# Issuing three kinds of transfers from GpSimd's queue instead of SyncE's

## The chip, the cores and the metric

The kernel runs on one core of a Trainium2 chip. The metric is the device time of one execution in microseconds (us), as the median of several runs. The engines are named as in the profile: PE is TensorE (matrix multiply), PEld its weight load, DVE is VectorE, ACT is ScalarE, POOL is GpSimd and SP is SyncE. SP does no arithmetic here; it only issues transfers. ACT and POOL can issue transfers too, each on a queue of its own. SBUF is the core's on-chip memory, PSUM the small memory that PE writes to, and "DRAM" means the chip's large memory.

## The reference

The input x is 4 images of 512 channels, each 64 by 64 (f32). Two layers follow each other.

```python
# layer 0: linear attention with 64 heads of 8, with and without a convolution of q, k, v
qkv = concat(h @ wq.T, h @ wk.T, h @ wv.T)               # 1x1 projections, per pixel
pw  = grouped_1x1(depthwise_5x5(qkv))                    # a second set of q, k, v
f   = concat(qkv, pw).reshape(B, -1, 24, N)              # 128 heads, N = 4096 pixels
query, key_, value = relu(f[:, :, :8]), relu(f[:, :, 8:16]), f[:, :, 16:]
scores = einsum('bhdn,bhen->bhde', value_with_a_row_of_ones, key_)
out = einsum('bhde,bhen->bhdn', scores, query)
out = out[:, :, :-1] / (out[:, :, -1:] + EPS)            # divided by the row of ones
y = conv1x1(out, proj_kernel) * inv + shift + x

# layer 1: edge filters on y, four branches, attention over channels, fuse, norm, gelu
E = stack(sobel(y), laplace(y), diagonals(y), gradient(y))
feat = gelu(bn(einsum('kbchw,koc->bkohw', E, w_branch)))          # 4 x 128 channels
att = sigmoid(gelu(mean_hw(feat) @ w_att1.T + b_att1) @ w_att2.T + b_att2)
z = conv1x1(feat * att, w_fuse) + b_fuse
z = (z - mean_c(z)) / sqrt(var_c(z) + eps)
result = gelu(z * ln_gamma + ln_beta) + y
```

## The kernel before, in words

**The front.** For each of the 4 images there are 4 groups of 128 channels (class `Group`, 16 groups). A group makes keys, values and queries of 8 strips of 512 pixels each (`project`, L256, and `values`, L279), their attention scores, the 5 by 5 convolutions of keys and queries (`convolve`, L388, 160 small matmuls per half), and a correlation that replaces the convolution of values (`correlate`, L441). The queries are not multiplied with the scores here. They are divided by their denominators on DVE (`divide`, L378, tile `q`; `conv_divide`, L548, tile `cq`) and stored in the DRAM tensors `heads` and `cheads`, 256 KB at a time. The matrices of a convolution are built on POOL (`load_mat`, L236, tile `mat`, two buffers).

**The three stages behind.** When all four groups of an image are done, three generators work it off. `project_out` (L612, called Y below) loads the divided queries again (tile `hd`), multiplies them with the folded projection, adds x, and writes y to DRAM. `edge_branches` (L667, called E) loads windows of y (tile `win`), forms the edge maps on DVE and ACT, multiplies them with the branch weights and stores the result as `ef`. `fuse_out` (L759, called F) loads `ef` in 8 strips, four tiles of 128 channels to a strip. For each channel tile `c` its helper `fuse` (L805) does four matmuls (L808), a square on ACT (L810), the tile `z` on DVE (L812, six buffers) and, for three of four, a running sum on POOL (`total`, L815). Its helper `norm` (L817) sums the squares over channels on PE (L819), takes root and reciprocal (L821, L822), and then for each of the four tiles: loads the rows of y that are added to the result (tile `yr`, two buffers), multiplies (L829, DVE), applies gelu (L830, ACT), adds `yr` (L833, POOL), and stores the result in `out` (L834).

**What sets the order.** PE's instructions run in the order in which the program issues them (`manual_schedule`, L101). Into that order the stages behind are mixed by hand: `advance` (L881) is called after each step of the front with that step's share of time, and pulls steps of Y, E and F of the image before. So F of images 0, 1 and 2 has the front, or E of the last image, beside it, and F of image 3 stands alone at the end. In `norm`'s place in the strip loop,

```python
fuse(0, ef, zs, total)
fuse(1, ef, zs, total)
norm(j - 1, *held)
fuse(2, ef, zs, total)
fuse(3, ef, zs, total)
```

two `z` tiles of the new strip exist before the four of the old one are stored, which fills the six buffers. The third and fourth `z` of a strip can be written only when the first two stores of the strip before have landed. The other engines and queues get their order at build time, by dependences and program order. A queue works its list from the front: a transfer that waits for its data holds back all that stand behind it. Transfers wait, too, for the landing of earlier and unrelated ones on the same queue, as the waits of SP show.

Of the kernel before, what the change touches and what calls it, by code (L numbers as in the profile page):

```python
# [83 lines left out]
def conv_seq_kernel(  # L84
    ctx: ExitStack, tc, x, wqkv, dpk, wtab, proj, projc, pwk, bn0, consts, vec, watt1, batt1, watt2, wbr, wfuse, out
):
    nc = tc.nc
# [15 lines left out]
    def work_tile(name, n=512):  # L103
        return work.tile([P, 512], F32, tag="w", name=name)[:, :n]

    def ps_tile(name):
        return psum.tile([P, 512], F32, tag="ps", name=name)
# [8 lines left out]
    def rows(ap, width=W):  # L116
        return ap.rearrange("p (r c) -> p r c", c=width)
# [79 lines left out]
    def center_bias():  # L197

        fb_ps = ps_tile("fb_ps")
        nc.tensor.matmul(fb_ps[:, 0:4], lhsT=ones, rhs=vec_sb[:, V_FB, :], start=True, stop=True)  # L200
        fb_mean = const.tile([P, 1], F32, name="fb_mean")
        nc.vector.tensor_reduce(fb_mean, fb_ps[:, 0:4], AX.X, ALU.add)
        nc.vector.tensor_scalar(fb_mean, fb_mean, 1.0 / C, None, ALU.mult)
        nc.vector.tensor_scalar(fbias, vec_sb[:, V_FB, :], fb_mean, None, ALU.subtract)
# [15 lines left out]
    class Group:  # L220
# [157 lines left out]
        def divide(self, half):  # L378
            banks = self.spread_out(self.rec)
            for k in range(4):  # L380
                j = 4 * half + k
                q = work_tile("q")
                nc.vector.tensor_mul(q, self.rq.pop(j), banks[k])
                nc.sync.dma_start(out=self.heads[j, :, self.g, :], in_=q)

# [160 lines left out]
        def conv_divide(self, half):  # L548
            banks = self.spread_out(self.crec)
            for i in range(4):  # L550
                q = work_tile("cq")
                nc.vector.tensor_mul(q, self.conv[QUERY][i], banks[i])
                nc.sync.dma_start(out=self.cheads[half, self.g, i], in_=q)

# [202 lines left out]
    def fuse_out(b, efs, pool_sb, side):  # L759

        y = ys[b % 2]
        with ExitStack() as stack:
            pool = stack.enter_context(tc.tile_pool(name=f"F{b}", bufs=2, side=side, reuse_waits="tile"))
            wf_sb = pool.tile([P, NCH, C], F32, name="wf_sb", bufs=1)
            nc.sync.dma_start(out=wf_sb, in_=wfuse)
            watt1_sb = pool.tile([P, NCH, 64], F32, name="watt1_sb", tag="sq", bufs=3)
            nc.sync.dma_start(out=watt1_sb, in_=watt1)
            watt2_sb = pool.tile([64, C], F32, name="watt2_sb", tag="sq", bufs=3)
            nc.sync.dma_start(out=watt2_sb, in_=watt2)
            wf_mean = small.tile([P, NCH], F32, name="wf_mean")  # L770
            nc.vector.tensor_reduce(wf_mean, wf_sb, AX.X, ALU.add)
            nc.vector.tensor_scalar(wf_mean, wf_mean, 1.0 / C, None, ALU.mult)
            yield 0.0


            pooled = small.tile([P, 4], F32, name="pooled")
            nc.vector.tensor_reduce(pooled, pool_sb, AX.X, ALU.add)
            yield 14.0
            if b == 0:
                center_bias()  # L780
            hid_ps = ps_tile("hid_ps")
            for k in range(4):
                nc.tensor.matmul(
                    hid_ps[0:64, 0:1], lhsT=watt1_sb[:, k, :], rhs=pooled[:, k : k + 1], start=(k == 0), stop=(k == 3)
                )
            hid = small.tile([64, 1], F32, name="hid")
            nc.scalar.activation(hid, hid_ps[0:64, 0:1], AF.Gelu, bias=batt1_sb, scale=1.0 / N)
            yield 4.0
            att_ps = ps_tile("att_ps")
            for k in range(4):  # L790
                nc.tensor.matmul(att_ps[:, k : k + 1], lhsT=watt2_sb[:, ts(k, P)], rhs=hid, start=True, stop=True)
            att = small.tile([P, 4], F32, name="att")
            nc.vector.tensor_add(att, att_ps[:, 0:4], vec_sb[:, V_ATT2, :])
            nc.scalar.activation(att, att, AF.Sigmoid)

            for k in range(4):
                nc.vector.tensor_scalar(
                    wf_sb[:, k, :], wf_sb[:, k, :], wf_mean[:, k : k + 1], att[:, k : k + 1], ALU.subtract, ALU.mult
                )
            yield 8.0  # L800


            share = SHARE_F / (NJ * 5)

            def fuse(c, ef, zs, total):  # L805
                ps = ps_tile("zps")
                for k in range(4):
                    nc.tensor.matmul(ps, lhsT=wf_sb[:, k, ts(c, P)], rhs=ef[k], start=(k == 0), stop=(k == 3))  # L808
                sq = total if c == 0 else pool.tile([P, 512], F32, name="sq", tag="sq", bufs=3)
                nc.scalar.activation(sq, ps, AF.Square, bias=fbias[:, c : c + 1])  # L810
                z = pool.tile([P, 512], F32, name="z", tag="z", bufs=6)
                nc.vector.tensor_scalar(z, ps, fbias[:, c : c + 1], None, ALU.add)  # L812
                zs.append(z)
                if c:
                    nc.gpsimd.tensor_add(total, total, sq)  # L815

            def norm(j, zs, total):  # L817
                ps = ps_tile("var")
                nc.tensor.matmul(ps, lhsT=ones, rhs=total, start=True, stop=True)  # L819
                rstd = pool.tile([P, 512], F32, name="rstd", tag="rstd", bufs=1)  # L820
                nc.scalar.activation(rstd, ps, AF.Sqrt, bias=ln_eps, scale=1.0 / C)  # L821
                nc.vector.reciprocal(rstd, rstd)  # L822
                for c in range(NCH):
                    z = zs[c]
                    yr = pool.tile([P, 8 * WB], F32, name="yr", tag="yr")
                    nc.sync.dma_start(
                        out=yr, in_=y[c].rearrange("p r w -> p (r w)")[:, (8 * j + 1) * WB : (8 * j + 9) * WB]
                    )
                    nc.vector.tensor_mul(z, z, rstd)  # L829
                    nc.scalar.activation(  # L830
                        z, z, AF.Gelu, bias=vec_sb[:, V_LNB, c : c + 1], scale=vec_sb[:, V_LNG, c : c + 1]
                    )
                    nc.gpsimd.tensor_add(rows(z), rows(z), rows(yr, WB)[:, :, 1 : W + 1])  # L833
                    nc.sync.dma_start(out=out[b, c, :, ts(j, 512)], in_=z)  # L834

            held = None
            for j in range(NJ + 1):
                if j < NJ:
                    ef = []
                    for k in range(4):  # L840
                        t = pool.tile([P, 512], F32, name="ef", tag="ef", bufs=8)
                        nc.sync.dma_start(out=t, in_=efs[j][:, k, :])
                        ef.append(t)
                    zs = []
                    total = pool.tile([P, 512], F32, name="total", tag="total")
                    fuse(0, ef, zs, total)
                    yield share
                    fuse(1, ef, zs, total)
                    yield share
                else:  # L850
                    yield 6.0
                if held:
                    norm(j - 1, *held)
                    yield share
                if j < NJ:
                    fuse(2, ef, zs, total)
                    yield share
                    fuse(3, ef, zs, total)
                    yield share
                    held = zs, total  # L860
# [191 lines left out]
```

## Time and profile before

| | before |
|---|---|
| median of 3 runs | 5078.56 us (5077.92 to 5086.61) |
| the profiled execution: its own time | 5063.71 us |
| its span, first to last instruction | 5061.9 us |
| granted clock of TensorE, mean | 0.967 |
| PE busy | 4702.0 us (93%) |
| DVE busy | 2124.7 us (42%) |
| ACT busy | 1626.5 us (32%) |
| POOL busy | 392.7 us (8%), 291 instructions |
| transfers issued by SP, by ACT | q1: 758.68 MB, q10: 100.74 MB |
| F of image 0, 1, 2, 3, about | 1816 to 2070, 3140 to 3390, 4600 to 4870, 4910 to 5062 us |

The busy time of an engine is the time in which it ran instructions. A row of waits says which instruction waited, for whom, how long in total, how many times, and the longest wait. The timeline gives instructions in order of time, with the idle time before them in square brackets. Issuing a transfer is not counted as busy time; the queue SPq has rows of its own.

### The profile page before, as it was taken

The page shows a single profiled execution, that of the slowest core. Times are in us where ns is not written, and L with a number is a line of the kernel's source. Part 1 is how long each engine was busy: PE and PEld are TensorE (multiplying, and loading weights), DVE is VectorE, ACT ScalarE, POOL GpSimd, SP SyncE. Part 2 cuts the span into 40 slices and gives each one's busy share as a digit, 9 for nine tenths or more (in the row PEclk, how much of TensorE's full clock was granted, in tenths as well). Part 3 has the DMA queues.
Part 4 walks back from the last instruction along what each step waited for, and adds up shares of the span by engine and source line. Part 5 has one row for each costly group of instructions (what it writes and reads, how often), then busy time and mean ns, then how long its engine had stood idle before and what let it go on. Part 6 is the DMA issues. An engine that isn't in the chain of part 4 may idle for free. (4 is left out here: it accounts for less than half of the span.)

```text
span 5061.9 us, 107134 instructions
## 1 busy us (share of the span) xinstructions
PE 4702.0 (93%) x46362; PEld 2739.7 (54%) x46362; DVE 2124.7 (42%) x2960; ACT 1626.5 (32%) x2833; POOL 392.7 (8%) x291
## 2 busy tenths in 40 slices
PE   9999999999999999799899999899989898898777
PEld 5665654455666554454465655454456665445443
DVE  1222221116556433211455653431146557157965
ACT  2112111004444423200345442320024445035765
POOL 0000000000000013100000000310000000001335
PEclk9999999999999999899999999999999999999889
DMA  6444466666656565676555665657655553774425
GB/s 196 138 123 130 132 206 190 158 165 181 192 189 183 179 205 170 197 178 156 176 176 181 193 202 176 213 188 167 163 173 175 184 169 129 200 184 118 151 88 172
DMA packets 635945, 866.26 MB, mean 171 GB/s; under 512 B 324393, under 2 KB 395081, under 8 KB 617041
## 3 DMA queue, kind: packets, MB, share of 16 engines
q1 hardware_dynamic: 551504, 758.68, 51.8%
q10 hardware_dynamic: 83968, 100.74, 6.4%
q8 instruction: 364, 5.96, 0.5%
q14 instruction: 109, 0.88, 0.1%
HBM read 578.09 MB, written 213.98 MB: 156 GB/s over the span
## 5 line engine op out<-in xcount | busy, mean ns | idle before, releaser
L262 PE MATMUL proj<-xt,w_sb 128*128 128x512 f32 x2048 | 955.8, 610 | 52.9 <-DMA xt<-in_x 31.8
L655 PE MATMUL yps<-hd,fold_sb 128*128 128x512 f32 x2048 | 899.6, 596 | 9.7 <-DMA hd<-heads 8.7
L396 PE MATMUL cv<-inp,mat 32*32 32x512 f32 x20480 | 730.2, 597 | 35.4 <-issue 27.3
L262 PEld LDWEIGHTS proj<-xt,w_sb 128*128 128x128 f32 x2048 | 382.7, 194 | 523.3 <-issue 450.7
L655 PEld LDWEIGHTS yps<-hd,fold_sb 128*128 128x128 f32 x2048 | 384.9, 190 | 493.5 <-issue 445.3
L396 PEld LDWEIGHTS cv<-inp,mat 32*32 32x32 f32 x20480 | 420.3, 103 | 314.6 <-issue 154.2
L730 PE MATMUL br<-maps,wbr_sb 128*128 128x256 f32 x2048 | 495.0, 396 | 51.8 <-ACT maps L713 42.2
L808 PE MATMUL zps<-ef,wf_sb 128*128 128x512 f32 x1024 | 469.9, 610 | 53.5 <-DMA ef<-ef 19.0
L730 PEld LDWEIGHTS br<-maps,wbr_sb 128*128 128x128 f32 x2048 | 399.7, 198 | 165.9 <-issue 51.3
L284 PEld LDWEIGHTS val<-w_sb,xt 128*128 128x128 f32 x4096 | 470.2, 192 | 33.9 <-issue 26.1
L284 PE MATMUL val<-w_sb,xt 128*128 128x128 f32 x4096 | 484.9, 277 | 0.6 <-DVE vt L291 0.3
L660 DVE SCALAR_TENSOR_TENSOR yt<-yps,shift,xr 128x512 f32<-128x512 f32 x128 | 96.1, 750 | 871.8 <-PE yps L655 788.9
L268 ACT COPY strip<-proj 128x512 f32<-128x512 f32 x256 | 149.1, 582 | 928.5 <-PE proj L262 910.4
L451 PE MATMUL corr<-near,ckt 128*32 128x160 f32 x8192 | 333.6, 315 | 35.0 <-DMA near<-near 28.4
L808 PEld LDWEIGHTS zps<-ef,wf_sb 128*128 128x128 f32 x1024 | 196.1, 195 | 296.6 <-issue 235.6
L241 POOL TENSOR_TENSOR mat<-dp_sb 128x1280 f32<-128x1280 f32 x32 | 77.2, 2414 | 3464.5 <-PE cv L396 2951.0
L451 PEld LDWEIGHTS corr<-near,ckt 128*32 128x32 f32 x8192 | 256.9, 111 | 131.5 <-issue 73.1
L703 DVE TENSOR_TENSOR maps<-dv 128x1054 f32<-128x1054 f32 x128 | 162.6, 1271 | 366.9 <-PE br L730 366.9
L312 ACT ACTIVATE kt<-tr 128x512 f32<-128x512 f32 x128 | 75.8, 593 | 528.9 <-PE tr L310 345.9
L737 ACT ACTIVATE ef_o<-br,shift,scale 128x256 f32<-128x256 f32 x256 | 142.3, 559 | 283.5 <-PE br L730 251.9
L360 DVE RECIPROCAL rec<-rec 128x512 f32<-128x512 f32 x64 | 214.4, 3350 | 1.7
L812 DVE TENSOR_SCALAR z<-zps,fbias 128x512 f32<-128x512 f32 x128 | 94.9, 744 | 283.4 <-DMA out<-z 97.0
(125 smaller groups left out, 4135.7 us busy)
## 6 DMA issues: line engine op xcount, KB each, us to landing
xt<-in_x SPq DMA_DIRECT2D x316, 512.0 KB
near<-near SPq DMA_DIRECT2D x512, 264.0 KB
inp<-strip ACTq DMA_DIRECT2D x1024, 64.0 KB
win<-y SPq DMA_DIRECT2D x128, 396.0 KB
near<-vt SPq DMA_DIRECT2D x512, 66.0 KB
y<-yt SPq DMA_DIRECT2D x128, 264.0 KB
yr<-y SPq DMA_DIRECT2D x128, 264.0 KB
heads<-q SPq DMA_DIRECT2D x128, 256.0 KB
```

Of the source, the lines that this page charges most:

```text
L262: nc.tensor.matmul(ps, lhsT=self.w[t][:, c, :], rhs=xs[self.b, j][c], start=(c == 0), stop=(c == NCH - 1))
L268: nc.scalar.copy(s, ps)
L284: nc.tensor.matmul(ps[:, ts(c, P)], lhsT=xs[self.b, j][n][:, ts(c, P)], rhs=self.w[VALUE][:, n, :], start=(n == 0), stop=(n == NCH - 1),)
L360: nc.vector.reciprocal(rec, rec)
L396: nc.tensor.matmul(rows(banks[i])[32 * j : 32 * j + 32, :, c0:c1], lhsT=self.mat[t][q, j, (dx + 2) * 8 + 4 * b : (dx + 2) * 8 + 4 * b + 4, :],
L451: nc.tensor.matmul(self.banks[jj][32 * i : 32 * i + 32, 160 * b : 160 * b + 160], lhsT=self.held["c", i][:, at : at + 32], rhs=v[:, 4 * n ...
L655: nc.tensor.matmul(ps, lhsT=fold_sb[g // NG][:, g % NG, ts(c, P)], rhs=hd[g], start=(g == 0), stop=(g == 2 * NG - 1),)
L660: nc.vector.scalar_tensor_tensor(yt[:, :, 1 : W + 1], rows(ps), shift0[:, c : c + 1], rows(xr), ALU.add, ALU.add)
L703: nc.vector.tensor_sub(flat[:, half : 3 * half - 2], dvs[:, 2 : 2 * half], dvs[:, 0 : 2 * half - 2])
L730: nc.tensor.matmul(rows(ps)[:, 4 * n : 4 * n + 4, :], lhsT=wbr_sb[:, k, c, :], rhs=rows(maps[c // 2][:, slot[k], c % 2, :], WB)[:, :, 0:W] ...
L737: nc.scalar.activation(o[:, n, :], ps[:, 256 * n : 256 * n + 256], AF.Gelu, bias=shift1[:, k : k + 1], scale=scale1[:, k : k + 1], accum_o ...
L808: nc.tensor.matmul(ps, lhsT=wf_sb[:, k, ts(c, P)], rhs=ef[k], start=(k == 0), stop=(k == 3))
```

## The change

Four lines get another engine as issuer; nothing else is edited. The stores of divided queries (L384, L553), the loads of the rows of y in F (L826) and the stores of the results (L834) go from SP's queue to POOL's. Each kind is issued 128 times in the run, 512 in all: 256 KB for the three stores, 264 KB for the load.

```diff
@@ divide
                 nc.vector.tensor_mul(q, self.rq.pop(j), banks[k])
-                nc.sync.dma_start(out=self.heads[j, :, self.g, :], in_=q)
+                nc.gpsimd.dma_start(out=self.heads[j, :, self.g, :], in_=q)
@@ conv_divide
                 nc.vector.tensor_mul(q, self.conv[QUERY][i], banks[i])
-                nc.sync.dma_start(out=self.cheads[half, self.g, i], in_=q)
+                nc.gpsimd.dma_start(out=self.cheads[half, self.g, i], in_=q)
@@ fuse_out, norm
-                    nc.sync.dma_start(
+                    nc.gpsimd.dma_start(
                         out=yr, in_=y[c].rearrange("p r w -> p (r w)")[:, (8 * j + 1) * WB : (8 * j + 9) * WB]
                     )
...
                     nc.gpsimd.tensor_add(rows(z), rows(z), rows(yr, WB)[:, :, 1 : W + 1])
-                    nc.sync.dma_start(out=out[b, c, :, ts(j, 512)], in_=z)
+                    nc.gpsimd.dma_start(out=out[b, c, :, ts(j, 512)], in_=z)
```

## The prediction

> **What bounds the kernel now.** I read the page first. PE is busy nearly everywhere except in the last three of 40 slices, and POOL works only where an F stage runs:
>
> ```profile
> PE   9999999999999999799899999899989898898777
> DVE  1222221116556433211455653431146557157965
> POOL 0000000000000013100000000310000000001335
> ```
>
> So up to about 4570 us the change can help only where PE waits for a load that SP issues late; from there on it can also hurt. Next the waits of SP's queue. These rows hold what the change takes away:
>
> ```profile
> SPq L834 <- POOL z L833: 291.5, 123, 18.1
> SPq L384 <- DVE q L383: 90.3, 75, 10.2
> SPq L553 <- DVE cq L552: 87.7, 84, 20.3
> ```
>
> SP stands still for 291.5 us until POOL has added `yr`, and for 178.0 us until DVE has divided; all loads behind stand still with it. Does PE notice? The waits of PE, asked stretch by stretch, show loads as the cause in few places. From 1800 to 2200 us (F of image 0) and from 3100 to 3450 us (F of image 1):
>
> ```profile
> PE proj L262 <- DMA xt<-in_x: 17.0, 1, 17.0
> PE corr L451 <- DMA near<-near: 9.7, 1, 9.7
> ```
> ```profile
> PE zps L808 <- DMA ef<-ef: 19.0, 1, 19.0
> PE corr L451 <- DMA near<-near: 3.3, 1, 3.3
> PE proj L262 <- DMA xt<-in_x: 2.0, 1, 2.0
> ```
>
> That is 51.0 us in the two F stages. Elsewhere before 4570 us such rows sum to 36.8 us (6.8, 3.3, 0.5, 17.6 and 8.6 in five stretches). In F of image 2 (4600 to 4870 us) no PE wait names a load, and DVE is busy for 252.2 of 270 us: it bounds that stage. F of image 3 stands alone. Its timeline, one strip, without the weight loads:
>
> ```profile
> 5006.48 2.78 POOL L833 TENSOR_TENSOR z<-z,yr 128x512 f32<-128x512 f32 x2 [0.55 <-ACT z L830]
> ...
> 5008.16 1.47 SPq L834 DMA_DIRECT2D out<-z  x2
> ...
> 5009.68 0.91 SPq L826 DMA_DIRECT2D yr<-y  x2
> 5010.26 0.75 DVE L812 TENSOR_SCALAR z<-zps,fbias 128x512 f32<-128x512 f32 x1 [3.18 <-DMA out<-z]
> ...
> 5011.07 1.12 PE L819 MATMUL var<-total,ones 128*128 128x512 f32 x2 [0.70 <-DVE z L812]
> ...
> 5012.93 1.18 POOL L833 TENSOR_TENSOR z<-z,yr 128x512 f32<-128x512 f32 x1 [3.66 <-issue]
> ...
> 5022.60 2.54 POOL L833 TENSOR_TENSOR z<-z,yr 128x512 f32<-128x512 f32 x2 [0.80 <-ACT z L830]
> ```
>
> The strip returns after 5022.60 - 5006.48 = 16.1 us. The store of the first result is issued at 5008.16 and lands 2.1 us later; only then can DVE write the third `z`, free a PSUM bank, and let PE go on (0.70 us late). Here the landing of `out` is already on the path.
>
> **The price of an issue on POOL.** No transfer of before goes by POOL. SP issues one in 0.34 us (the store's median), which is one end. POOL's own instructions over 128 partitions take 1.18 us (`z` plus `yr`, undisturbed), 1.27 us (`total`) and 2.39 us (`mat`); the last is the other end. I take 1.2 us: the `z` add is POOL's nearest row, the same tile that the store then describes row by row. POOL cannot add meanwhile, so this counts against POOL's other work.
>
> **The change, part by part.** All is reckoned against the profiled execution's 5063.71 us (span 5061.9 and 1.8 around it); the median of the runs is 14.85 us higher, and I carry the difference over.
>
> *Divided queries, 256 stores.* POOL gets 256 x 1.2 = 307 us over 4340 us in which it is busy for 227 us: room enough. The stores queue behind `mat` (waiting for PE's convolution) and `total` (waiting for ACT); `heads` is read a stage later, and no wait of PE names a lack of work tiles, so a late store costs nothing. If that cover failed, a `q` held back by `mat` would cost some of SP's longest wait for `mat`, 17.0 us, once per image: up to 68. SP, all told, waits 3475 us; the 178.0 taken away are 5%, and 5% of 36.8 is 2; SP's issues there (256 x 0.33 = 84 us) add as much again at most. I take -4; ends -37 and +68.
>
> *`yr` and `out` in F of images 0 and 1: gain.* In the SP timeline of image 0, SP waits from 2059.34 to 2064.85 for a sum while the next `near` load, for which PE stands 9.7 us, is behind it: -5.5. The `xt` stall follows in the same burst of loads, which begins earlier by as much as PE does, so it stays. In image 1 two stores and two loads stand ahead of nine `near` loads that begin at 3273.55 and ahead of the missing `ef`; without them the burst begins after 3268.35 + 0.66 = 3269.0: -4.5. Sum -10; ends 0 and -51.
>
> *The same, loss.* The second store is now issued after one more issue (1.2) and its own price (1.2 instead of 0.34): about 2 us later. DVE waited for `out` there 24 times (25.8 + 32.6 us), and the PE waits that name `z` sum to 6.4 us, 0.11 per us. 24 x 2 x 0.11 = +5; ends 0 and +48, all of it.
>
> *F of image 2.* POOL's eight strips cost 8 x 18.1 us (worked out next) of 270 us: no bound. DVE waited only 1.5 us for `out`, so stores had slack; I let half of the strips meet the 2 us: 8 x 0.5 x 2 = +8. Ends: the 69.4 us that SP waited there for sums hid no load that anybody waited for, so 0 below; +28 above, 3.5 us on every strip.
>
> *F of image 3.* Per strip POOL has four adds (4.7), three sums (3.8) and now eight issues (9.6): 18.1 us. The `var` matmuls start at 4933.09, 4947.68, 4962.27, 4978.54, 4995.07, 5011.07, 5026.93 and 5038.01: two periods of 14.6 us, when PE alone bounds, four of 16.2 on average, and a short last one. With POOL as the bound: 2 x 3.5 + 4 x 1.9 = 15, and before the last landing stand two more issues and a dearer store: +3. Sum +18. At SP's price a strip costs POOL 11.2 us and nothing is lost; at 2.39 us it costs 27.6 us, 2 x 13.0 + 4 x 11.4 = 72, with 8 for the end +80.
>
> Together: -4 - 10 + 5 + 8 + 18 = +17. Profiled execution 5080.7, median 5078.56 + 17 = 5095.6.
>
> **Two rules against the trace.** SP stood 305 us in front of L834 against 128 x 0.34 = 43 us of issuing, so most of what is taken away is waiting, and 10 us of it reached PE. The Trainium skill, DMA: Bandwidth & Descriptors, section "Issuing engines are not separate DMA queues", says that issuing from several engines saves only the issuing sequencer's time; taken strictly, the two gains vanish and the sum is +31. And POOL's adds, 1.18 us undisturbed, took 1.67 to 1.83 us beside DVE's two-input instructions in F of image 2, where DVE is fullest. The skill's SBUF — State Buffer, section "Who interferes with whom", says that VectorE in a two-port mode locks GpSimd out, and the box before it has such a transfer take 3.1 us instead of 0.62; as an estimate from that page, were half of a tail strip's issues hit, 4 x 2.5 x 6 strips = 60 us would come on top: +77.
>
> **The rivals.** *Faster: SP's freed queue decides.* If an issue on POOL costs under (14.6 - 8.5) / 8 = 0.76 us, the tail pays nothing, and the freed queue returns half of the 51 us of load stalls: 5078.56 - 25 = 5053. For it: 305 us of SP's waits sit before L834, exactly where `ef`, `near` and `xt` come late. Against it: the bursts behind those waits take 10 us and more by themselves.
>
> *Much slower: POOL's issue costs as much as `mat`.* At 2.39 us the tail alone loses 80 us; with +8, +5 and -14 elsewhere, +79: about 5158. For it: a transfer's 128 rows on two sides are many small pieces of work. Against it: `mat` writes 1280 elements per partition, far more than a list of rows.
>
> *Nothing to measure.* At about 0.9 us a strip costs 15.7: 2 x 1.1 + 3 = 5 in the tail, +8 and +5 before, -14 gained: 5083.
>
> **How the numbers follow.** About 0.2% (10 us) is what a measurement of this kernel can tell from no change. The forecast (slower by some 17 us) gets 0.47, the faster rival 0.27, no difference 0.15, much slower 0.11. Faster is the first rival: 0.27; same 0.15; slower 0.47 + 0.11 = 0.58. The range reaches down to 5045, past most of the faster rival, and up to 5150, short of the much slower one: it leaves out some 0.08 below and 0.11 above. The slower cases alone would span 5089 to 5150.
>
> **What would show it.** POOL's rows of `out` and `yr` should last about 1.2 us; the `var` matmuls of the tail should stand about 18 us apart; SP's waits at L384, L553 and L834 should be gone; the 9.7 and 19.0 us waits of PE should be shorter by about 5. I am wrong if the tail keeps its periods of 14.6 and 16 us (I priced an issue too high), or if PE's waits in F of images 0 and 1 grow: then the order of POOL's list, sums and adds behind issues, costs more than the list's length.

## The result, and the profile after

The changed kernel took 5082.97 us (median of 12 runs, 5072.83 to 5094.65), the kernel before, run beside it, 5078.53 us (12 runs, 5072.4 to 5092.93). The ratio is 1.0003, with a 95% interval of 0.9991 to 1.0015: no difference that can be measured. The profiled execution took 5080.47 us, its span is 5078.7 us at a mean granted clock of 0.968.

That does not mean that nothing happened. The three rows of the busy engines first, 40 slices of the span each:

```profile
PE   9999999999999999899899999999989997998776
DVE  1222221116556433211565553431155566167965
POOL 0000000000000024200000002420000000002346
```

PE's dent in the slice from 2025 to 2151 us is smaller (7 became 8), and POOL's digits in the F stages rose. POOL was busy for 654.3 us instead of 392.7, with 512 more instructions. The waits of SP's queue (line, releaser, total us, times, longest):

```profile
SPq L253 <- PE proj L262: 372.2, 113, 23.1
SPq L683 <- DVE maps L706: 364.0, 62, 23.1
SPq L842 <- PE zps L808: 265.0, 77, 69.2
```

The rows of L834, L384 and L553, 469.5 us together, are gone. But these three rows were 283.2, 263.8 and 134.3 us before: they rose by 320 us together, as waits for buffers to come free. Where SP no longer stood for POOL or DVE it stood for something else. What PE noticed of it, from 1800 to 2200 us and from 3100 to 3450 us:

```profile
PE ctr L423 <- ACT ckt L425: 14.5, 1, 14.5
PE val L284 <- DVE z L812: 5.4, 1, 5.4
PE cden L543 <- DVE z L812: 3.4, 1, 3.4
```
```profile
PE yps L655 <- DMA hd<-heads: 7.0, 1, 7.0
PE den L366 <- DVE z L812: 3.1, 1, 3.1
```

The load stalls shown before (17.0, 9.7 and 19.0 us among them) have left these rows, whole and not by 5 us each. (Why they went is read from SP's list below.) In F of image 0 others took their place: ACT (14.5) and `z` (5.4 + 3.4 = 8.8). In F of image 1 one shorter wait did, 7.0 us for the first load of Y. One strip of the tail, from its timeline (start, duration, engine, instruction, idle before):

```profile
4977.18 0.56 POOL L834 DMA_DIRECT2D out<-z  x1 [0.30 <-POOL z L833]
...
4977.76 1.19 POOL L833 TENSOR_TENSOR z<-z,yr 128x512 f32<-128x512 f32 x1
...
4978.89 0.57 POOL L826 DMA_DIRECT2D yr<-y  x1
...
4979.45 0.54 POOL L834 DMA_DIRECT2D out<-z  x1
4979.59 0.75 DVE L812 TENSOR_SCALAR z<-zps,fbias 128x512 f32<-128x512 f32 x1 [2.15 <-DMA out<-z]
...
4983.10 0.75 DVE L812 TENSOR_SCALAR z<-zps,fbias 128x512 f32<-128x512 f32 x1 [2.76 <-DMA out<-z]
...
4983.77 3.34 DVE L822 RECIPROCAL rstd<-rstd 128x512 f32<-128x512 f32 x1
4983.91 9.69 PE L808 MATMUL zps<-ef,wf_sb 128*128 128x512 f32 x18 [2.39 <-DVE z L812]
```

The second store follows a `yr` load in POOL's list: issued at 4979.45, 2.27 us after the first (before, the pair took 1.47 us on SP), and DVE writes the `z` that needs its landing at 4983.10. PE stands 2.39 us for that, where it stood 0.70 before. The reciprocal, and with it the rest of `norm`, is behind that waiting `z` in DVE's list. The `var` matmuls are 14.6, 16.6, 16.9, 19.0, 16.6, 18.8 and 11.7 us apart. And this is what an issue costs POOL (instructions by line; busy us in all, mean ns of one, then the idle time before them):

```profile
L826 POOL DMA_DIRECT2D yr<-y x128 | 71.0, 555 | 193.7 <-DMA y<-yt 105.0 <-DMA inp<-strip 64.0 <-DMA ef<-ef_o 11.9
L834 POOL DMA_DIRECT2D out<-z x128 | 70.8, 554 | 21.4 <-POOL z L833 20.8 <-DMA yr<-y 0.3 <-DMA inp<-strip 0.3
L384 POOL DMA_DIRECT2D heads<-q x128 | 69.8, 546 | 1184.9 <-DVE q L383 1152.6 <-DVE pooled L777 24.5 <-DVE dv L697 2.6
```

It is 0.55 us, not 1.2. A store right after its own add waits another 0.30 us for that add.

### The profile page after: what moved, and what is told of

It reads as the page before. It is cut to its first block, busy times and chain, and to the rows that moved or that the text cites. A ratio compares the mean times of both kernels' runs of the same rounds, so it can differ in the third digit from the quotient of the medians.

```text
span 5078.7 us, 107428 instructions
## 1 busy us (share of the span) xinstructions
PE 4704.0 (93%) x46362; PEld 2744.1 (54%) x46362; DVE 2133.4 (42%) x2960; ACT 1626.7 (32%) x2833; POOL 654.3 (13%) x803
## 3 DMA queue, kind: packets, MB, share of 16 engines
q1 hardware_dynamic: 477776, 623.38, 44.1%
q0 software_dynamic: 40960, 135.30, 7.6%
## 4 chain that ended last, share of the span: by engine, by line
PE 71%; issue 8%; DMA 8%; DVE 7%; ACT 3%; POOL 3%; ACTq 0%; SPq 0%; POOLq 0%; DVEq 0%
PE yps L655 17%; PE proj L262 13%; PE cv L396 11%; PE val L284 8%; PE br L730 6%; PE zps L808 5%; PE corr L451 4%; DMA near<-near 1%; DMA inp<-strip 1%; POOL z L833 1%; PE over L375 1%; PE tr L310 1%; DMA out<-z 1%; DVE maps L703 1%; PE s L321 1%
## 5 line engine op out<-in xcount | busy, mean ns | idle before, releaser
L262 PE MATMUL proj<-xt,w_sb 128*128 128x512 f32 x2048 | 947.9, 606 | 28.5 <-DVE vt L291 10.2
L655 PE MATMUL yps<-hd,fold_sb 128*128 128x512 f32 x2048 | 901.4, 597 | 16.9 <-DMA hd<-heads 15.5
L703 DVE TENSOR_TENSOR maps<-dv 128x1054 f32<-128x1054 f32 x128 | 166.0, 1297 | 371.0 <-PE br L730 371.0
L553 POOL DMA_DIRECT2D cheads<-cq x128 | 69.8, 545 | 1547.9 <-DVE cq L552 1538.1
L384 POOL DMA_DIRECT2D heads<-q x128 | 69.8, 546 | 1184.9 <-DVE q L383 1152.6
## 6 DMA issues: line engine op xcount, KB each, us to landing
win<-y SPq DMA_DIRECT2D x128, 396.0 KB
heads<-q POOLq DMA_DIRECT2D x128, 256.0 KB, 5.3
```

Of the source, the lines that this page charges most:

```text
L262: nc.tensor.matmul(ps, lhsT=self.w[t][:, c, :], rhs=xs[self.b, j][c], start=(c == 0), stop=(c == NCH - 1))
L655: nc.tensor.matmul(ps, lhsT=fold_sb[g // NG][:, g % NG, ts(c, P)], rhs=hd[g], start=(g == 0), stop=(g == 2 * NG - 1),)
L703: nc.vector.tensor_sub(flat[:, half : 3 * half - 2], dvs[:, 2 : 2 * half], dvs[:, 0 : 2 * half - 2])
```

## The experiments

The kernel before ran beside each group of kernels on the same chip. Its median was 5078.9 us in the group of the first four kernels below, 5058.5 beside the three of the queries and images 0 and 1 and beside `out` alone, 5077.9 (one run) beside those with more buffers and `yr` alone, and 5058.8 beside the last. So gains are given as ratios, or in us against the median of the same group. The repeat of before, the two kernels with more buffers and the two halves of the tail were run once each. The table gives stretches of the profiled executions in us. F0: from the `fold` matmul (L350) near 1720 us to Y's first matmul for image 1; F of image 0 lies in it. Ahead of F1: from there to the first `var` of image 1. F1: from that to Y's first matmul for image 2. F2: first to last `var` of image 2. Tail: seven periods of `var` in F of image 3. End: from the start of the last to the last instruction. In brackets stands the sum of PE's waits in the stretch.

| | F0 | ahead of F1 | F1 | F2 | tail | end |
|---|---|---|---|---|---|---|
| before | 396.7 (42.7) | 1030.7 (43.4) | 255.8 (27.0) | 231.4 | 104.9 | 23.9 |
| before, once more | 392.8 (41.9) | 1033.5 (47.7) | 255.5 (28.0) | 231.8 | 105.8 | 24.0 |
| after | 396.2 (43.8) | 1027.4 (43.1) | 238.9 (9.3) | 241.5 | 114.2 | 32.2 |
| one store on POOL | 392.5 (41.4) | 1043.4 (49.2) | 256.3 (27.5) | 231.9 | 105.5 | 24.2 |
| tail alone on POOL | 392.0 (41.1) | 1042.3 (48.2) | 254.1 (25.8) | 229.7 | 114.2 | 29.7 |
| after, tail on SP | 396.5 (39.7) | 1028.7 (42.7) | 236.7 (9.4) | 239.5 | 105.6 | 23.5 |
| queries alone | 374.3 (27.8) | 1027.0 (40.6) | 256.2 (27.7) | 230.7 | 105.0 | 25.4 |
| images 0, 1 alone | 384.2 (33.5) | 1031.4 (42.8) | 238.6 (11.0) | 231.9 | 104.9 | 24.4 |
| queries, images 0, 1 | 394.7 (38.0) | 1023.3 (38.3) | 236.1 (8.6) | 230.3 | 105.2 | 27.6 |
| queries, image 1 | 370.7 (28.4) | 1024.0 (42.5) | 239.0 (8.4) | 230.9 | 104.7 | 31.1 |
| after, more buffers | 396.0 (39.3) | 1028.4 (44.3) | 239.4 (9.3) | 240.8 | 110.9 | 27.3 |
| before, more buffers | 392.1 (39.9) | 1040.8 (50.2) | 252.6 (26.0) | 232.0 | 100.7 | 19.8 |
| tail, `out` alone | 384.6 (38.6) | 1035.7 (48.0) | 256.0 (27.8) | 231.2 | 125.5 | 21.8 |
| tail, `yr` alone | 393.2 (42.0) | 1037.4 (51.4) | 256.0 (27.3) | 231.8 | 120.9 | 21.1 |

How far can a column be trusted? Seven of these kernels issue nothing differently before 4900 us, but for one store and for the buffers of Y. Their F0 lies between 384.6 and 396.7, their stretch ahead of F1 between 1030.7 and 1043.4; their sums of waits lie closer, 38.6 to 42.7 and 43.4 to 51.4. So in these two stretches I read the waits, in the others the times.

**The kernel before, once more.** No edit.

> The kernel before, profiled a second time. Theory A (gains and losses by stage cancel): its last stretch, from the first lone `var` matmul of image 3 to the last `var`, is again about 105 us, and from there to the end about 24 us; F of image 1 (first `var` to the start of the next Y) again about 256 us; single stages repeat within some 4 us. Theory B (the stage differences between the two profiles are scatter of single executions): these stretches differ from the first profile of before by as much as the profile after does, 8 to 17 us.

Measured 5080.59 us. The profile of before shown at the top was 15 us under its own median; this one is near it (span 5078.8). Of the 17 us between the two, 12 lie in a stretch that is in no column, from Y of image 2 to Y of image 3. From F1 on the columns agree within 1 us.

**One store on POOL.**

```diff
-                nc.sync.dma_start(out=self.heads[j, :, self.g, :], in_=q)
+                (nc.gpsimd if self.b == 0 and self.g == 0 and j == 4 else nc.sync).dma_start(out=self.heads[j, :, self.g, :], in_=q)
```

> The kernel before, with a single store of divided queries (image 0, group 0, strip 4) on POOL's queue and the other 511 transfers where they were. It asks what the first use of that queue costs by itself. Theory A: the closing drain of POOL takes some 7.8 us instead of 1.7, so the end comes some 5 us later than in before (+5 us in all); nothing else moves. Theory B: the drain's length in the profile after came from the 512 transfers or from the late landing of the last stores, so here it is 1.7 us and the time is that of before.

Measured 5082.67 us, ratio 1.0007 (0.9999 to 1.0016). The question was the end. POOL closes with an instruction called DRAIN. After (min/median/max ns, then first and last start):

```profile
L1048 POOLq DRAIN  x3: 45/102/7842, 5070.1 to 5078.4; - x3
```

The longest of the three takes 7842 ns here, 1712 in before and 1833 with one store. One use of the queue does not make the drain long; the theory of a fixed price falls.

**The tail alone on POOL, and the change without the tail.** In both only L826 and L834 differ from before or after:

```diff
-                    nc.sync.dma_start(                                    # e2, from before: L826 and L834
+                    (nc.gpsimd if b == B - 1 else nc.sync).dma_start(
-                    nc.gpsimd.dma_start(                                  # e3, from after: L826 and L834
+                    (nc.sync if b == B - 1 else nc.gpsimd).dma_start(
```

> The kernel before with only `yr` and `out` of image 3 (64 transfers, the stage that stands alone) on POOL's queue. Theory A: +18 us, slower by 0.35%: the seven periods between `var` matmuls sum to about 114 us instead of 105 and the end from the last `var` is about 32 us instead of 24. Theory B: no difference, within 0.1%.

> The kernel after with only `yr` and `out` of image 3 back on SP's queue; divided queries and F of images 0 to 2 stay on POOL's. Theory A: the tail returns to about 105 + 24 us but for the closing drain of about 5 us; against before -7 to -13 us (faster by 0.15 to 0.25%), about 15 us better than after. Theory B: no difference from before.

The tail alone: 5096.82 us against 5078.9, ratio 1.0037 (1.0024 to 1.005). The change without it: 5061.09 us, ratio 0.9956 (0.9943 to 0.9969). So the change is a loss of about 18 us in the tail and a gain of about as much elsewhere, more than the 7 to 13 us expected. The tail's columns go up by 9 and 6 us in the first and return to 105.6 and 23.5 in the second.

**The queries alone, and images 0 and 1 alone.**

```diff
-                nc.sync.dma_start(out=self.heads[j, :, self.g, :], in_=q)      # e4: L384, and L553 alike
+                nc.gpsimd.dma_start(out=self.heads[j, :, self.g, :], in_=q)
-                    nc.sync.dma_start(                                    # e5: L826 and L834
+                    (nc.gpsimd if b < 2 else nc.sync).dma_start(
```

> The kernel before with only the divided queries (256 stores) on POOL's queue. The gain of some 22 us that after has ahead of its last stage must come from these stores or from F of images 0 and 1. Theory A (the gain is made in F, where SP stood in front of results that POOL had not added): within 5 us of before, and F of image 1 keeps its 256 us. Theory C (the gain is made by the divided queries, which hold SP in the front): -10 us or more, spread over the front, and F of image 1 down to about 240 us.

> The kernel before with only `yr` and `out` of images 0 and 1 (128 transfers) on POOL's queue. Theory A: F of image 1 falls from 256 to about 239 us and its 19 us wait of PE for `ef` is gone; -17 us or more in all (faster by 0.35%). Theory C: no difference from before beyond 5 us, F of image 1 keeps 256 us.

The queries alone took 5031.6 us against 5058.47: ratio 0.9946 (0.9927 to 0.9966), some 27 us, by far the largest part, from the edit priced at -4. Theory C had the size; but F of image 1 kept its 256 us, as theory A had it. Images 0 and 1 alone: 5042.61 us, 0.9965 (0.9952 to 0.9978). PE's waits from 1800 to 2200 us, the queries alone:

```profile
PE corr L451 <- DMA near<-near: 11.6, 1, 11.6
```

The 17.0 us for `xt` are gone, the wait for `near` remains. SP's timeline shows what became of that load. Before, then with the queries alone:

```profile
2077.18 10.87 SPq L436 DMA_DIRECT2D near<-near  x11
2088.65 0.35 SPq L253 DMA_DIRECT2D xt<-in_x  x1
```
```profile
2033.01 0.42 SPq L253 DMA_DIRECT2D xt<-in_x  x1
...
2068.64 15.56 SPq L436 DMA_DIRECT2D near<-near  x11
```

The order of SP's list has changed at build time, though the edit names no load: the `xt` load stood behind these eleven `near` loads and five earlier ones, and now stands ahead of all sixteen. Of the 14 profiles, the seven in which it stands behind have the stall (16.7 to 18.3 us), the seven in which it stands ahead have none. It is the same with the 19 us for `ef` in F of image 1: in eight profiles, the queries alone among them, the fourth `ef` load of a strip stands behind sixteen `near` loads, and PE waits 18.6 to 19.7 us; in the six with F of image 1 on POOL it stands ahead of them, and the wait is gone. No run moves the transfers and holds the order of the loads.

With images 0 and 1 alone, the window from 1800 to 2200 us:

```profile
PE ctr L423 <- ACT ckt L425: 13.8, 1, 13.8
PE cden L543 <- DVE z L812: 2.8, 1, 2.8
```

Here the `xt` stall is gone and that for `near` is 1.6 us, but ACT's 13.8 us stand in their place. Each edit alone removes the `xt` stall. By the sums of waits in F0 the queries bring 13 us (some 41 to 27.8), images 0 and 1 bring 8 (to 33.5); in F1 the second edit brings 17 more.

**Queries with images 0 and 1.** Both edits above, images 2 and 3 on SP.

> The kernel after with `yr` and `out` of images 2 and 3 back on SP's queue: POOL issues the divided queries and F of images 0 and 1. Theory A: the 10 us that F of image 2 lost (241 instead of 231 us) come back on top of the tail's 18, so against before about -27 us (faster by 0.55%), the best of all. Theory B' (the loss in F of image 2 is not due to its transfers but to the order that the front leaves behind): no better than the kernel with the tail alone put back, -18 us.

Measured 5039.89 us against 5058.47, 0.9961 (0.9949 to 0.9973): 19 us, where 27 + 16 = 43 is the sum of the parts. F1 keeps its gain (8.6 us of waits); F0 is back at 38.0, with neither the 13 us of the one nor the 8 of the other. The F2 column is back at 230.3, as theory A had it; but the ratio is no better than the 0.9956 (0.9943 to 0.9969) of the kernel with the tail alone put back, so the 10 us of F2 are seen in the column and not in the whole time. The trace names the new wait. In the kernel after, ACT's own list around it:

```profile
2093.94 0.60 ACT L273 ACTIVATE rq<-proj 128x512 f32<-128x512 f32 x1
...
2105.52 4.45 ACTq L277 DMA_DIRECT2D inp<-strip  x4
2110.07 1.56 ACT L425 COPY ckt<-ctr 128x512 f32<-128x512 f32 x3 [15.52 <-DMA inp<-strip]
2110.71 1.11 PE L423 MATMUL ctr<-consts_sb,co 128*128 128x128 f32 x4 [14.46 <-ACT ckt L425]
```

ACT had the queries ready at 2094.54, but its four stores of them (L277, ACT's queue) are issued only at 2105.52. Behind them in ACT's list stands the copy that PE needs. The stall on SP's loads has become a stall behind ACT's stores. In the same time SP issues 17 loads in one burst (2093.01 to 2111.80). The trace's semaphore events show what the stores waited for: each starts within 0.07 us of the landing of one of that burst's `near` loads (2105.45, 2106.71, 2108.05 and 2109.47), which it does not use. And the burst itself began late. SP's waits after, from 2050 to 2100 us:

```profile
SPq L637 <- DMA out<-z: 16.8, 1, 16.8
```

SP stood in front of Y's second load until the last `out` store of image 0 had landed, which POOL issued at 2090.58; SP had issued it at about 2066 in before. All five kernels with F of image 0 on POOL show this wait of SP (14.8 to 16.8 us) and PE's wait for ACT's copy (11.9 to 14.5); in the nine other profiles SP waits there for that store 0.6 us at most, and PE for `ckt` 2.7 at most. Why the store comes so late was not tested; POOL's adds ahead of it wait 9.7 and 4.4 us for `yr`. Then there is `z`: DVE's wait for `out` from 1800 to 2070 us is 52.8 us after (before 25.8), and 50.8 in this kernel between 1715 and 2120; with the queries alone it is 21.7.

**Queries with image 1 only.** If the tail and F of image 0 and 2 lose or gain nothing on POOL, they can stay on SP:

```diff
-                    nc.gpsimd.dma_start(                                  # from after: L826 and L834
+                    (nc.gpsimd if b == 1 else nc.sync).dma_start(
```

> The kernel before, with the 256 divided-query stores on POOL in the whole run and `yr` and `out` on POOL in F of image 1 alone; images 0, 2 and 3 keep them on SP. Theory A (the parts stand in different stages and add, as long as F of image 0 is left alone): the stretch with F of image 0 takes some 374 us as with the queries alone (before 393 to 397), the stretch with F of image 1 some 238 us (before 256), the stretch ahead of F of image 1 some 7 us less than before; together about -45 us, a ratio near 0.991. Rival B (the lists are coupled by the order made at build time, so that a gain in one stage is lost in another, as with queries and images 0 and 1 together): the stretch of image 0 is back at 393 to 397 us or that of image 1 at 256; about -20 to -27 us, a ratio of 0.995 to 0.996.

Measured 5023.89 us (5017.99 to 5025.69, 5 runs) against 5058.82: ratio 0.993, interval 0.9917 to 0.9944. It is the fastest version, 35 us under the kernel before. PE's waits from 1800 to 2200 us hold one load, and the wait for ACT is short:

```profile
PE corr L451 <- DMA near<-near: 11.8, 1, 11.8
PE ctr L423 <- ACT ckt L425: 2.7, 1, 2.7
```

PE's waits are 28.4 us in F0 and 8.4 in F1, the gain of the queries and that of image 1 side by side, as theory A had it; B would have had one of the two back. With the 5 us or so ahead of F1 they sum to 13 + 5 + 19 = 37. A's 45 us had been taken from the times of the stretches and not from the waits. The end column gives back 7: POOL's drain took 10.5 us here, and 9.7 us pass from the end of the last add to the last instruction (before 3.1).

**More buffers in the tail.** Eight `z` buffers in F of image 3 instead of six, paid for by `hd` and `xr` buffers of Y of image 3:

```diff
-                z = pool.tile([P, 512], F32, name="z", tag="z", bufs=6)            # L811, in after (e6) and in before (e7)
+                z = pool.tile([P, 512], F32, name="z", tag="z", bufs=8 if b == B - 1 else 6)
-                    t = pool.tile([P, 512], F32, name="hd", tag="hd", bufs=11 if side == "right" else 10)
+                    t = pool.tile([P, 512], F32, name="hd", tag="hd", bufs=11 if side == "right" else 9)
-                    xr = pool.tile([P, 512], F32, name="xr", tag="xr", bufs=3)
+                    xr = pool.tile([P, 512], F32, name="xr", tag="xr", bufs=3 if side == "right" else 2)
```

> The kernel after with eight instead of six `z` buffers in the tail (to make room, the Y stage of image 3 has 9 instead of 10 `hd` and 2 instead of 3 `xr` tiles, so Y may be a little slower; only the tail is read). With eight, a new strip's third and fourth tile need not wait for the stores of the strip before. If the landing of `out` is what lengthens the tail's periods, the seven sum to about 103 us, PE's 14.7 each, and the waits of DVE for `out` vanish. If POOL's list is the bound, they stay at 114.

> The kernel before with the same eight `z` buffers in the tail (and the same 9 `hd` and 2 `xr` tiles in the Y stage of image 3). If the landing of `out` was already on the path in before, the seven periods fall from 105 to about 103 us; if not, they stay.

From after: 5081.92 us, tail 110.9 instead of 114.2, end 27.3 instead of 32.2. From before: 5080.09 us, tail 100.7, end 19.8: 4 us less each, so the landing of `out` was on the path before too. The gap between the two, 10.2 us in the tail and 7.5 at the end, is about as large as without the buffers (9.3 and 8.3). So the landing alone is not the tail's loss; 110.9 us is what neither the 103 nor the 114 of the expectation had. From 4900 to 5100 us in after with more buffers:

```profile
PE var L819 <- POOL total L815: 13.8, 6, 7.8
```

The wait for `z`, 7.7 us after, is gone, and 13.8 us for POOL's sum stand instead (3.3 after): the sums are behind adds and issues in POOL's list. Relieve one, and the other is late.

**One half of the tail at a time.**

```diff
-                    nc.sync.dma_start(                                    # e9: L834 only; e10: L826 only
+                    (nc.gpsimd if b == B - 1 else nc.sync).dma_start(
```

> The kernel before with only the stores `out` of image 3 on POOL's queue; its `yr` loads stay on SP's. The seven periods between the `var` matmuls of the tail sum to 105 us in before and 114 with both kinds on POOL. Theory P (the price of an issue and the later landing of a store on POOL's queue make the loss): still 111 or more. Theory Q (the loss is made by the load `yr` that stands ahead of the second store in POOL's list and on the queue): 105 to 107, and the end shorter than 30 us.

> The kernel before with only the loads `yr` of image 3 on POOL's queue; its stores stay on SP's. Theory P (the stores' own price and landing on POOL's queue make the tail's loss): the seven periods sum to 105 to 107 us. Theory Q (the load in POOL's list is what delays): 110 or more, as the add of a strip's second tile and its store no longer follow at once.

`out` alone: 5075.09 us, tail 125.5, end 21.8. `yr` alone: 5089.71 us, tail 120.9, end 21.1. 125.5 meets theory P's "111 or more" and 120.9 theory Q's "110 or more", so each half costs by itself. Either costs more in the periods than both (114.2), but the end is shorter: tail and end together are 147.3 and 142.0 us, against 146.4 with both and 128.8 before. Half of the move costs about as much as the whole, which none of the theories had. With `out` alone, one strip:

```profile
4995.13 0.75 DVE L812 TENSOR_SCALAR z<-zps,fbias 128x512 f32<-128x512 f32 x1 [3.41 <-DMA out<-z]
...
4996.31 1.02 PE L819 MATMUL var<-total,ones 128*128 128x512 f32 x2
...
5003.72 3.34 DVE L822 RECIPROCAL rstd<-rstd 128x512 f32<-128x512 f32 x1
```

From the start of `var` to that of its reciprocal pass 7.4 us (3.4 in the strip of after shown above), because DVE has more `z` tiles to write first, which wait for landings or for ACT: in both of these kernels six stand ahead of a reciprocal in DVE's list where four do before and after. With `yr` alone, PE waits 14.3 us for `total`. So the issuing engine also decides the order that each list gets at build time; how much of the loss is order and how much is issues these runs do not separate.

## Why the prediction was wrong in its parts and right in its range

The forecast was +17 us and the measurement is within 0.15% of nothing; the rival "nothing to measure", at 5083, is the number that came out. But it came out for another reason than the rival gave, and that it lies in the range is in part luck: the queries were missed by 23 us one way, and F of image 0 the other way. The step under most of the misses is that the prediction took every list to keep its order, but for the transfers that move; the build gave SP, POOL and DVE new ones.

**The price of an issue: mis-sized.** 1.2 us was taken from an add; it is 0.55 us, 1.6 times SP's 0.34 and under the 0.76 us at which I had the tail pay nothing. A strip costs POOL 8.5 + 8 x 0.55 = 12.9 us of its 14.6 us: the length of POOL's list is not the bound.

**The tail: right in size, wrong in cause.** I said +15 in the periods and +3 at the end; the columns say +9 and +8, and the tail alone costs 18 us. The failed step here is "at SP's price a strip ... and nothing is lost": it looked at the length of POOL's list and not at its order. What the trace shows is the second store behind a `yr` load, `z` behind its landing, the reciprocal behind `z`, and, with more buffers, the sums behind issues. The prediction named order as a way to be wrong, but not with a price. Of the end's 8 us, 6 come after the last add: 8.9 us from its end to the last instruction, 3.1 before.

**The queries: the step that cost most.** I priced -4 (ends -37 and +68), by taking 5% of SP's waits as 5% of the lost PE time. Alone they gain 27, of which PE's waits show 13 in F0 and 3 to 11 ahead of F1. A share of an average is the wrong measure: one stall went whole, the 17.0 us of `xt`. I wrote that it "stays", because its burst begins earlier by as much as PE does; with either edit alone the row is gone, because the load is no longer in that burst. It did not stand behind a waiting store of queries either: the last four of them before it were issued by 2044.88, the load at 2088.65 behind eleven `near` loads.

**F of images 0 and 1: mis-sized both ways.** I said -10 and +5. Image 1's stretch gains 17, not 4.5: I let the burst with the `ef` load begin earlier, but the build put that load ahead of the burst, and its wait vanished whole. (For `near` in image 0 I read a wait of 5.5 us; SP was issuing until 2060.00, so it was 4.8.) Image 0's gains nothing in the full change, since the new ACT wait of 14.5 and `z` waits of 8.8 us take what `xt` and `near` gave up (26.7). For the loss I had DVE wait 48 us more for `out`, at 0.11 us of PE for each. It waited 27.0 more in image 0 and 28.1 more in image 1 (32.6 to 60.7), 55 together; the PE waits that name `z` there rose from 6.4 to 16.7 us. So this term is +10 where I had +5; what I had not reckoned at all is that Y's loads wait for the last `out` store, and ACT's stores for the burst behind them.

**F of image 2: right in size, half in cause.** +8 said, +10 in the column. DVE's wait for `out` rose from 1.5 to 5.4 us, and DVE was busy for 230.5 us of the stretch instead of 224.9: 3.9 + 5.6 = 9.5 us. The second part I had not foreseen. Of DVE's rows L703 went up, from 1362 to 1541 ns, and L697 down, from 853 to 696; why was not tested.

**The sum.** Against the profile of before that lies near the median, and whose span is 0.1 us longer than after's: F0 +3, ahead of F1 -6, F1 -17, F2 +10, tail +8, end +8, that is +6, and -6 in what lies between. The measured ratio is worth +1.5 us (-4.6 to +7.6). The parts by themselves give -27 (queries), -16 (images 0 and 1), +10 (F2) and +18 (tail), that is -15. What is lost between -15 and +1.5 is, by PE's waits, F0: its stalls can go once, and when both edits meet there the new waits take as much as the stalls gave.

**The two rules.** Issuing from another engine brought 0.9946 with the queries alone, which is 27 us, where 256 issues by 0.33 us are 84 us of SP's time. The Trainium skill, DMA: Bandwidth & Descriptors, section "Issuing engines are not separate DMA queues", taken strictly gave +31 and no gain; the gain measured here is against that sum. How much of it is SP's time for the issues, how much its waits and how much the new order of its list no run separates. POOL's issues took 539 to 580 ns for `out` and 546 to 571 for `yr` in the whole run, beside DVE's fullest stage too. The lock of SBUF — State Buffer, section "Who interferes with whom", that gave +77 does not show in this kernel's rows; whether DVE was ever in the mode that takes it no row tells. (The 3.1 and 0.62 us stand on that page not in the box but in a paragraph after it, for a transfer beside a `tensor_copy`.)

**What remains open.** What the queries' gain and that of image 1 would be with the loads in their old order. Why the last `out` store of image 0 comes so late from POOL. Why DVE's rows change in F of image 2. Why the drain varies so. What part of the tail's loss is build order and what is the price of the issues: an order held fixed by hand was not tried.

## What to carry to other kernels

Where the order of the lists is made at build time, naming another issuer is also a new order: build the change, read the new list around each stall of the bounding engine, and only then price it. Here the two largest stalls went whole because one load each stood ahead of a burst instead of behind it, and a new one came from a load that waited for a late store on the other queue. Gains in one stretch do not add when they remove the same stall, so decide the engine stage by stage; here, of what was tried, it was best to leave `yr` and `out` of three of the four images alone. Before putting a store on an engine that also computes, read what is in front of it in that engine's list, and what waits for its landing.

## What the runs showed of the hardware that was not expected

An issue of 128 rows on POOL lasts 0.55 us with hardly any spread, and moves a quarter of a megabyte. The transfers also changed in packets: 512 of them were 73728 packets on SP's queue (551504 less 477776) and are 40960 on POOL's, with the same 135.3 MB.

POOL's DRAIN at the end was longer wherever its queue had been used for more than one transfer, but it does not follow their count: 1.8 us after 1, 3.7 and 3.9 after 32, 5.9 after 64, 3.5 after 128, 5.3 after 256, 10.5 after 320, 7.1 after 384, 3.5 after 448 and 7.8 after 512. With the queries and image 1, where it takes 10.5 us, the end is 7 us longer than before.

A transfer can wait for one of another queue that it does not use: the four stores of ACT at 2105.52 to 2109.49 started 0.02 to 0.07 us after the landing of `near` loads that SP had issued. By the trace the store and the load in each pair signal the same semaphore; that the build hands them out so is read from this trace alone.
